# Two gated Flamingo layers in fp32: the place of a weight fold, the order of pools, the norms of the last layer and the order of two stores

## Chip, cores and metric

The kernel runs on one core of a Trainium2 chip. The metric is the time of one execution on the device in microseconds (us); lower is better. The time before is 3406.6 us, the median of three runs. All data is fp32.

## The reference, cut

`x` is 8 x 256 x 1024, `ctx` likewise. Each of four sublayers is added to `x` through a tanh gate, after a layer norm of `x`:

```python
x = x + tanh(g_xattn[0]) * L0_xattn(layernorm(x), ctx, ctx)
x = x + tanh(g_ffn[0])   * L0_ffn(layernorm(x), W, b, A, B, gate_w, gate_b)
x = x + tanh(g_xattn[1]) * L1_xattn(layernorm(x), ctx, ctx, mask, wq, wk, wv, wo)
x = x + tanh(g_ffn[1])   * L1_ffn(layernorm(x), W_base, b_base, enc0, enc1, coefs0, coefs1, mask0, mask1)

# L0_xattn: autocorrelation over 8 heads of 128 channels
qf, kf = fft(q, axis=seq), fft(k, axis=seq)
corr = ifft(qf * conj(kf)).real                  # per channel, 256 lags
w, idx = top_k(corr over lags, 11); w = softmax(w)
out = sum_i w[i] * v[min(idx[i] + pos, L - 1)]

# L0_ffn: x W^T + b, plus a LoRA path whose rank (8, 16, 32 or 64) a gate picks per token (top 1)

# L1_xattn: grouped-query attention, 32 query heads, 8 heads of keys and values, rope, mask, softmax

# L1_ffn: base linear plus 0.5 * sum over 3 experts of a real inverse Fourier
# transform of (x enc0^T) w0^T + (x enc1^T) w1^T; all of it is linear in x
```

## The kernel before

**Passes and sublayers.** The kernel makes two passes (`p` = 0 and 1) over four batches each. A pass holds its x in eight tiles of 128 x 1024 (`xt`) and runs through `autocorrelation`, `lora_ffn`, `attention` and `fourier_ffn`. Products of matrices are computed with seven block products in place of eight (`SEVEN`), so there are sums of operands (L158 on POOL or DVE, L206 to L209) and additions of results (`combine`, L220 to L250; `add_product`, L252 to L274; `residual`, L371) besides the matmuls.

**Autocorrelation.** The loop takes eight turns, one for each batch and half of the channels, and a last one that only ends the eighth. A turn transforms its half of the context and of the normalized x with matmuls against a constant (`dft<-...`, L412), multiplies spectra (L428 to L431 on DVE, then L432 to L436 on POOL), transforms back (`ps_cor`, L562 and L563) and picks the eleven best lags on DVE (`lags`, L574 to L587). POOL adds and subtracts the two halves of the weights (`both`, L553). The next turn turns these over with PE (`pt<-ident,both`, L513), transforms them (L412), multiplies them with the spectrum of the values, and adds the result to x (`po`, L532, and `residual` L371). So in each turn there is the front half of one piece and the back half of the one before.

**What runs beside it.** PE would often wait in these turns, so the turn calls `fill(n)`, which pulls n steps from the generator `beside()` (L1167). Its steps are pieces of other work, mostly matmuls: `keys_values(n)` for the two blocks of 512 context tokens of the pass (56 steps each: matmuls L798 for k and v from the weights `wk` and `wv` and the context tiles `cx`, whose sums `cx_t` are formed on POOL at L158 for block 1), and in pass 0 `fold_last_layer` (17 steps). The fold makes one weight of the whole last sublayer: masked coefficients on DVE and POOL, eight steps of matmuls L302 with the Fourier matrix, then eight steps of matmuls L320 (40 rows deep), whose results are added to `w1` on DVE (L327), summed for the seven products (L333 to L336 on DVE) and stored to device memory (L332, L338). What steps are left after the last turn are run behind it (L1189). In pass 0 there are 129 steps; the turns pull 122 of them, and seven steps of the fold are left.

**Tiles and order.** The wide tiles lie in a pool of seven buffers for each of three tags (`a`, `b`, `xn`): weights, context tiles and the fold's operands share these buffers, and a load waits until the tile before in its buffer is done with. The other pools are opened by each stage; a later pool lies over the place of an earlier one, and with `reuse_waits="tile"` an instruction that writes a tile waits for the users of whatever tiles lay at that place. So the order in which a stage opens its pools sets which tiles of the next stage lie over which tiles of this one. Each engine works through its own list in order; SP issues the loads and direct stores, also in order. A scheduler puts the instructions into these lists, so calls that are moved in the code can also move others.

**The layer after it.** `lora_ffn` starts with its norms (`xn`, L356), transposes (L366, copies `xnT` L367 on ACT), the gate and LoRA product (`pa<-ag,xnT`, L625) and then the wide products (L669). Its operand `ag` is loaded at L1207.

**The last layer.** `fourier_ffn` (L1090) loads the folded weight, computes the statistics of all eight tiles (`norm_stats`: L349, L350, L351, L352), and then for pairs of tiles `m`: normalizes and transposes both (`prepare`), forms the operands' sums (`left`), and runs the seven products of the pair before (`project`, matmuls L1127). At the end of `project`, the even tile of x goes to the output with a direct store from SP (L1136), and the odd one with a scatter by row numbers from POOL (L1137). Both write the same output tensor, and the second of them waits for the first.

Of the kernel before, what the change touches and what calls it, by code (L numbers as in the profile page):

```python
# [19 lines left out]
P = 128  # L20
B, S, D = 8, 256, 1024
# [3 lines left out]
TT = BP * S // P  # L25
# [8 lines left out]
NBT = NB // P  # L34
# [12 lines left out]
def flamingo_kernel(ctx: ExitStack, tc: tile.TileContext, a: dict, out: bass.AP):  # L47
# [336 lines left out]
    def autocorrelation(p, xt, pools, beside, late):  # L384
# [88 lines left out]
        def turn(this, before, coming):  # L473


            after = None
            if this:
                b, cols, end, qe, qo, ke, ko = this
                if coming:
                    coming = loads(coming)  # L480
                kr_ps, ki_ps = dft((KCE, ke)), dft((KSE, ko), (NYQ, ke))


                kr, ki, kn = sb("kr"), sb("ki"), sb("kn")
                nc.scalar.copy(kr, kr_ps)
                nc.scalar.copy(kn, kr_ps)
                nc.scalar.activation(ki, ki_ps, AF.Copy, scale=pair)
                nc.scalar.copy(kn[0:1, :], ki_ps[0:1, :])
                re, im = sb("re"), sb("im")
                products(spectrum((CE, SE), (qe, qo)), kr, ki, kn, re, im, False)  # L490
                fill(2)

            if this:
                vr_ps, vi_ps = dft((KCO, ko)), dft((KSO, ke))
                vr, vi = sb("vr"), sb("vi")
                nc.scalar.copy(vr, vr_ps)
                nc.scalar.copy(vi, vi_ps)

                nc.vector.scalar_tensor_tensor(
                    kr[0:1, :], end[0:1, :], 2.0 * S, kr[0:1, :], ALU.mult, ALU.add  # L500
                )
                fill((1 if p == 0 else 2) if before else 6 if p == 0 else 2)
            last = not this
            if before:
                if last:
                    fill(3)
                b_cols, b_tiles, (bkr, bki, bkn, bvr, bvi, both) = before

                wt = []
                for t in range(2):  # L510
                    pt = ps_out.tile([P, HALF], F32, tag="out", name="pt")
                    for c in range(4):
                        nc.tensor.transpose(pt[:, c * P : (c + 1) * P], both[:, t, c, :], ident)  # L513
                    wt.append(one(f"wt{t}"))
                    nc.scalar.copy(wt[t], pt)
                    fill(2 if last else 1)
                er, ei = sb("re"), sb("im")
                products(spectrum((CE, SE), wt), bkr, bki, bkn, er, ei, True)
                fill(2 if last else 1)
                odr, odi = one("odr"), one("odi")  # L520
                products(spectrum((CO, SO), wt[::-1]), bvr, bvi, bvr, odr, odi, True)
                fill(3 if last else 2)
            if this and coming:
                after = sums(*coming)

            def back(l):


                if before:
                    po = ps_out.tile([P, HALF], F32, tag="out", name="po")  # L530
                    for i, (k, sp) in enumerate(((0, er), (3, odi)) if l else ((1, ei), (2, odr))):
                        nc.tensor.matmul(po, inv2[:, k, :], sp, start=(i == 0), stop=(i == 1))  # L532
                    residual(b_tiles[0][:, b_cols], po, tg_x[0])
                    residual(b_tiles[1][:, b_cols], po, tg_x[0] if l else ntg_x[0])
                    fill(1 - l)

            if last:
                back(0)
                back(1)
                return None, None  # L540
            w = big_tile("xn", [4, S], "w")
            cor = correlation(re, im, 0)
            fill(1)
            back(0)
            cor += correlation(re, im, 2)
            for c in range(2):
                lags(w[:, c, :], cor[c])
            fill(1)
            back(1)
            for c in range(2, 4):  # L550
                lags(w[:, c, :], cor[c])
            both = big_tile("xn", [2, 4, P], "both")
            nc.gpsimd.tensor_add(both[:, 0], w[:, :, 0:P], w[:, :, P:S])  # L553
            nc.gpsimd.tensor_sub(both[:, 1], w[:, :, 0:P], w[:, :, P:S])
            return after, (cols, xt[b * 2 : b * 2 + 2], (kr, ki, kn, vr, vi, both))
# [534 lines left out]
    def fourier_ffn(p, xt, groups):  # L1090
        with (
            tc.tile_pool(name="f1c", bufs=1, reuse_waits="tile") as w1,
            tc.tile_pool(name="f1", bufs=2, reuse_waits="tile") as w2,
            tc.tile_pool(name="f1_t", bufs=4, space=PSUM) as ps_t,
            tc.tile_pool(name="f1_o", bufs=4, space=PSUM) as ps_o,
        ):
            w = stored_weight(groups, lambda r: w1_d[WEIGHTS.index(r)])

            bias1 = w1.tile([P, D], F32, name="bias1")
            nc.sync.dma_start(bias1, a["b1"].partition_broadcast(P))  # L1100
            nc.vector.tensor_scalar(bias1, bias1, tg_f[1], None, ALU.mult)
            norms = [norm_stats(xt[i * NBT : (i + 1) * NBT]) for i in range(TT // NBT)]

            def prepare(t):
                xn = w2.tile([P, D], F32, tag="xn", name="xn")
                normed(xn, xt[t], *norms[t // NBT], t % NBT)
                xnT = w2.tile([P, KC, P], F32, tag="xnT", name="xnT")
                transposed(xnT, xn, ps_t, "t")
                return xnT

            def left(first, second):
                q = [[s[:, k * KH : (k + 1) * KH, :] for k in range(2)] for s in (first, second)]
                s = [w2.tile([P, KH, P], F32, tag=f"s{i}", name=f"s{i}") for i in (1, 2, 4)]
                return left_operands(nc.vector, q, *s)

            def project(m, ops):
                x = [
                    [xt[m * 2 + i][:, j * HALF : (j + 1) * HALF] for j in range(2)] for i in range(2)
                ]
                part = [w2.tile([P, HALF], F32, tag=f"part{i}", name=f"part{i}") for i in range(2)]  # L1120

                for i in range(2):
                    nc.vector.tensor_add(xt[m * 2 + i], xt[m * 2 + i], bias1)
                for r in SEVEN:
                    po = ps_o.tile([P, HALF], F32, tag="o", name="po")
                    for c in range(KH):
                        nc.tensor.matmul(  # L1127
                            po,
                            ops[r][:, c, :],
                            w[r].chunk(c),  # L1130
                            start=(c == 0),
                            stop=(c == KH - 1),
                        )
                    add_product(r, po, x, tg_f[1], ntg_f[1], part)
                b = p * BP + m
                nc.sync.dma_start(out[b * S : b * S + P, :], xt[m * 2])  # L1136
                nc.gpsimd.indirect_dma_start(  # L1137
                    out,
                    bass.IndirectOffsetOnAxis(ap=rows[:, b : b + 1], axis=0),
                    xt[m * 2 + 1],  # L1140
                    None,
                )

            pending = None
            for m in range(TT // 2):
                got = left(prepare(m * 2), prepare(m * 2 + 1))
                if pending is not None:
                    project(*pending)
                pending = (m, got)
            project(*pending)  # L1150

    for p in range(NPASS):
        ga, gb = ("a", "b") if p % 2 == 0 else ("b", "a")
        xt = [xpool.tile([P, D], F32, tag="x", name="x") for t in range(TT)]
        with (
            tc.tile_pool(name="kv1", bufs=1, reuse_waits="tile") as kw1,
            tc.tile_pool(name="kv2", bufs=2, reuse_waits="tile") as kw2,
            tc.tile_pool(name="ac1", bufs=1, reuse_waits="tile") as c1,
            tc.tile_pool(name="acw", bufs=1, reuse_waits="tile") as aw1,
            tc.tile_pool(name="ac2", bufs=2, reuse_waits="tile") as aw2,  # L1160
            tc.tile_pool(name="ac_dft", bufs=4, space=PSUM) as ps_dft,
            tc.tile_pool(name="ac_cor", bufs=1, space=PSUM) as ps_cor,
            tc.tile_pool(name="ac_out", bufs=1, space=PSUM) as ps_out,
# [3 lines left out]
            def beside():  # L1167
                for n in range(p * BP * S // NB, (p + 1) * BP * S // NB):
                    yield from keys_values(n, (ga, gb), (kw1, kw2, ps_kv))
                if p == 0:  # L1170
                    yield from fold_last_layer((ga, gb), (kw1, ps_kv))

            def load_x(tiles):
                for t in tiles:
# [182 lines left out]
```

## Time and profile before

| | |
|---|---|
| median of 3 runs | 3406.6 us (3405.16 to 3411.6) |
| the profiled execution | 3400.72 us |
| its span, first to last instruction | 3399.0 us |
| mean granted clock of TensorE | 0.989 |
| DMA, mean over the span | 126 GB/s |

PE is the engine for matmuls (PEld its weight loads, which overlap), DVE, ACT and POOL work on elements, SP issues DMAs. A row of a timeline gives start, duration, engine, line, operation, out<-in, the partitions and elements, how many instructions were joined, and in brackets how long the engine had been idle and what ended that. "PEclk" is the clock that PE was granted, in tenths of full speed (1.00 in windows is full). The costliest groups of the page, for the sizes of things:

```profile
L954 PE MATMUL po<-wo,oT 128*128 128x512 f32 x960 | 432.1, 593 | 0.0
L925 PE MATMUL ps_q<-xn,wq 128*128 128x256 f32 x1920 | 428.9, 379 | 0.0
L371 DVE SCALAR_TENSOR_TENSOR x<-po,tg,x 128x512 f32<-128x512 f32 x376 | 269.0, 745 | 201.3 <-PE po L954 70.6
```

The columns behind the bar are busy time in all, the mean duration of one in ns, and the engine's idle time just before them. Durations of matmuls overlap one another; their distance from start to start is what counts.

### The profile page before, as it was taken

The numbers are of one execution on the slowest core, as the hardware profiler recorded it, in microseconds if no ns is written. First come the engines' busy times: TensorE is split into PE (matmuls) and PEld (weight loads), VectorE is DVE, ScalarE is ACT, GpSimd is POOL, SyncE is SP. The second block draws the span as 40 slices with busy tenths as digits, with TensorE's granted clock in tenths as the row PEclk, the third lists the DMA queues.
The fourth block names the chain that finished last, engine by engine and source line by source line (L and its number), as shares of the span: only waits on it lengthen the run. The fifth ranks groups of instructions, "written<-read, shape, count | busy, mean of one in ns | idle before, by whom it ended". The sixth has DMA issues, their size and how long they took to land. (4 is left out here: it accounts for less than half of the span.)

```text
span 3399.0 us, 36938 instructions
## 1 busy us (share of the span) xinstructions
PE 3319.6 (98%) x12784; PEld 2281.0 (67%) x12784; DVE 2245.2 (66%) x4229; ACT 859.5 (25%) x2061; POOL 1355.3 (40%) x1211
## 2 busy tenths in 40 slices
PE   8999999999999999999999999999999999999998
PEld 6676456777667767775467766577767777776754
DVE  7787666877777766665657775566666666666662
ACT  1332111322232322222123321122222323222220
POOL 4655212434443443445345541123443443344432
PEclk9999899999999999999999999999999999999999
DMA  7533625333333333343164333143333333333411
GB/s 273 172 115 117 213 87 176 118 137 133 139 126 129 121 119 120 121 163 103 50 203 153 126 102 131 32 158 123 123 121 121 113 123 115 121 123 122 152 38 50
DMA packets 161864, 431.72 MB, mean 127 GB/s; under 512 B 21476, under 2 KB 56292, under 8 KB 161678
## 3 DMA queue, kind: packets, MB, share of 16 engines
q1 hardware_dynamic: 160526, 425.17, 37.1%
q0 software_dynamic: 1152, 4.19, 0.3%
q8 instruction: 102, 1.67, 0.2%
q14 instruction: 84, 0.69, 0.1%
HBM read 350.66 MB, written 78.64 MB: 126 GB/s over the span
## 5 line engine op out<-in xcount | busy, mean ns | idle before, releaser
L719 POOL TENSOR_TENSOR qT<-rope,rope 128x512 f32<-128x512 f32 x128 | 170.0, 1328 | 866.9 <-DVE rope L718 866.9
L954 PE MATMUL po<-wo,oT 128*128 128x512 f32 x960 | 432.1, 593 | 0.0
L925 PE MATMUL ps_q<-xn,wq 128*128 128x256 f32 x1920 | 428.9, 379 | 0.0
L371 DVE SCALAR_TENSOR_TENSOR x<-po,tg,x 128x512 f32<-128x512 f32 x376 | 269.0, 745 | 201.3 <-PE po L954 70.6
L925 PEld LDWEIGHTS ps_q<-xn,wq 128*128 128x128 f32 x1920 | 364.8, 190 | 50.4 <-PE po L678 0.5
L987 ACT ACTIVATE s<-s,nmx 128x256 f32<-128x256 f32 x512 | 255.9, 500 | 276.5 <-DVE nmx L984 276.0
L982 DVE COPY_PREDICATED s<-keep,ps_s 128x512 f32<-128x512 uint8 x256 | 186.2, 730 | 183.0 <-PE ps_s L973 179.6
L954 PEld LDWEIGHTS po<-wo,oT 128*128 128x128 f32 x960 | 177.4, 190 | 175.6 <-issue 170.5
L954 PE MATMUL po<-wo,oS 128*128 128x512 f32 x640 | 287.7, 592 | 0.3 <-DVE x L371 0.3
L925 PE MATMUL ps_q<-xn_t,wq 128*128 128x256 f32 x1280 | 285.6, 379 | 0.0
L1014 ACT COPY wT<-pt 128x512 f32<-128x512 f32 x256 | 138.2, 590 | 516.3 <-PE pt L1008 516.0
L925 PEld LDWEIGHTS ps_q<-xn_t,wq 128*128 128x128 f32 x1280 | 243.2, 190 | 33.0
L1019 PE MATMUL av<-wT,v 128*128 128x256 f32 x1024 | 247.7, 384 | 3.8 <-ACT wT L1014 3.6
L973 PE MATMUL ps_s<-kT,qT 128*128 128x256 f32 x1024 | 247.9, 379 | 0.0
L1019 PEld LDWEIGHTS av<-wT,v 128*128 128x128 f32 x1024 | 192.5, 191 | 79.2 <-issue 44.0
L996 DVE TENSOR_SCALAR s<-s,tot 128x256 f32<-128x256 f32 x512 | 219.6, 469 | 7.7
L981 POOL MEMSET s<- 128x512 f32 x256 | 129.9, 527 | 222.2 <-PE pt L1008 220.5
L954 PEld LDWEIGHTS po<-wo,oS 128*128 128x128 f32 x640 | 119.0, 190 | 136.6 <-issue 128.9
L973 PEld LDWEIGHTS ps_s<-kT,qT 128*128 128x128 f32 x1024 | 191.6, 190 | 25.3 <-DVE x L371 0.5
L258 POOL TENSOR_TENSOR x<-x,part 128x512 f32<-128x512 f32 x80 | 114.9, 1436 | 213.5 <-ACT part L257 193.6
L984 DVE TENSOR_REDUCE nmx<-s 128x2 f32<-128x512 f32 x256 | 175.0, 685 | 8.3
L716 DVE TENSOR_TENSOR rope<-c,tab_q 128x512 f32<-128x512 f32 x128 | 88.4, 691 | 125.8 <-POOL c L240 119.9
(255 smaller groups left out, 5599.4 us busy)
## 6 DMA issues: line engine op xcount, KB each, us to landing
wq<-in_wq_dram SPq DMA_DIRECT2D x104, 512.0 KB, 3.3
wo<-in_wo_dram SPq DMA_DIRECT2D x104, 512.0 KB, 3.5
wq<-wq_d SPq DMA_DIRECT2D x96, 512.0 KB, 3.2
wo<-wo_d SPq DMA_DIRECT2D x96, 512.0 KB, 3.2
w<-w_d SPq DMA_DIRECT2D x36, 512.0 KB, 4.7
wk<-in_wk_dram SPq DMA_DIRECT2D x26, 512.0 KB, 5.8
wv<-in_wv_dram SPq DMA_DIRECT2D x26, 512.0 KB, 4.4
wk<-wk_d SPq DMA_DIRECT2D x24, 512.0 KB, 4.4
```

The costliest lines, as they stand in the source:

```text
L371: nc.vector.scalar_tensor_tensor(xs, ps, g, xs, ALU.mult, ALU.add)
L719: nc.gpsimd.tensor_add(dst, t0, t1)
L925: nc.tensor.matmul(ps[:, l, :], wops[r][:, l, c, :], xo[r][:, c, :], start=(c == 0), stop=(c == KH - 1),)
L954: nc.tensor.matmul(po, ops[r][:, h, t * P : (t + 1) * P], wops[r][:, h, :], start=(h == 0), stop=(h == 1),)
L973: nc.tensor.matmul(ps[:, t, :], qT[i, n][:, l, t * P : (t + 1) * P], kT[:, n * S : (n + 1) * S], start=True, stop=True,)
L981: nc.gpsimd.memset(s, MASKED)
L982: nc.vector.copy_predicated(s, keep[b], ps)
L984: nc.vector.tensor_reduce(nmx, s, AX.X, ALU.max, negate=True)
L987: nc.scalar.activation(s[:, t, :], s[:, t, :], AF.Exp, bias=nmx[:, t : t + 1], accum_out=tot[:, t : t + 1],)
L996: nc.vector.tensor_scalar(s[:, t, :], s[:, t, :], tot[:, t : t + 1], None, ALU.mult)
L1014: nc.scalar.copy(wT[i], pt)
L1019: nc.tensor.matmul(av[:, i, :], kv[step][1][:, n * 2 + c, :], wT[i][:, c, :], start=(c == 0), stop=(c == 1),)
```

## The change

Four edits, in the order of the diff:

1. In `turn`, the number of steps that are pulled after the transforms of the values (L502) is 2 in turns with a piece before them, in pass 0 too (it was 1 there). In `beside()`, the fold comes behind the first block of keys and values instead of behind the second. So in pass 0 the turns pull 129 steps, and the fold's 17 are steps 57 to 73, which fall into the fourth and fifth turn; the second block has steps 74 to 129.
2. In `fourier_ffn`, the statistics are computed for a block of four tiles when the first of them is prepared, instead of for all eight tiles at the start.
3. In `project` of `fourier_ffn`, the scatter of the odd tile is called ahead of the direct store of the even one.
4. The two pools of the keys and values (`kv1`, `kv2`) are opened behind the three pools of the autocorrelation instead of ahead of them.

Lines behind L1102 of the new kernel have numbers that are larger by two (L1127 is L1129); L1136 and L1137 trade places (L1144 and L1138).

```diff
@@ -499,7 +499,7 @@
                 nc.vector.scalar_tensor_tensor(
                     kr[0:1, :], end[0:1, :], 2.0 * S, kr[0:1, :], ALU.mult, ALU.add
                 )
-                fill((1 if p == 0 else 2) if before else 6 if p == 0 else 2)
+                fill(6 if p == 0 and not before else 2)
             last = not this
             if before:
                 if last:
@@ -1099,9 +1099,11 @@
-            norms = [norm_stats(xt[i * NBT : (i + 1) * NBT]) for i in range(TT // NBT)]
+            norms = {}
 
             def prepare(t):
+                if t % NBT == 0:
+                    norms[t // NBT] = norm_stats(xt[t : t + NBT])
                 xn = w2.tile([P, D], F32, tag="xn", name="xn")
                 normed(xn, xt[t], *norms[t // NBT], t % NBT)
                 xnT = w2.tile([P, KC, P], F32, tag="xnT", name="xnT")
@@ -1133,13 +1135,13 @@
                 b = p * BP + m
-                nc.sync.dma_start(out[b * S : b * S + P, :], xt[m * 2])
                 nc.gpsimd.indirect_dma_start(
                     out,
                     bass.IndirectOffsetOnAxis(ap=rows[:, b : b + 1], axis=0),
                     xt[m * 2 + 1],
                     None,
                 )
+                nc.sync.dma_start(out[b * S : b * S + P, :], xt[m * 2])
@@ -1153,11 +1155,11 @@
         with (
-            tc.tile_pool(name="kv1", bufs=1, reuse_waits="tile") as kw1,
-            tc.tile_pool(name="kv2", bufs=2, reuse_waits="tile") as kw2,
             tc.tile_pool(name="ac1", bufs=1, reuse_waits="tile") as c1,
             tc.tile_pool(name="acw", bufs=1, reuse_waits="tile") as aw1,
             tc.tile_pool(name="ac2", bufs=2, reuse_waits="tile") as aw2,
+            tc.tile_pool(name="kv1", bufs=1, reuse_waits="tile") as kw1,
+            tc.tile_pool(name="kv2", bufs=2, reuse_waits="tile") as kw2,
@@ -1167,8 +1169,8 @@
             def beside():
                 for n in range(p * BP * S // NB, (p + 1) * BP * S // NB):
                     yield from keys_values(n, (ga, gb), (kw1, kw2, ps_kv))
-                if p == 0:
-                    yield from fold_last_layer((ga, gb), (kw1, ps_kv))
+                    if n == 0:
+                        yield from fold_last_layer((ga, gb), (kw1, ps_kv))
 
             def load_x(tiles):
```

## The prediction

> **What bounds the kernel now.** I read the page first (busy times, forty slices, chain), then PE's waits and the stretches around its idle time.
>
> ```profile
> PE 3319.6 (98%) x12784; PEld 2281.0 (67%) x12784; DVE 2245.2 (66%) x4229; ACT 859.5 (25%) x2061; POOL 1355.3 (40%) x1211
> PEclk9999899999999999999999999999999999999999
> ```
>
> PE is the bound; the change removes no matmul. So only PE's waits and its slow clock can move the time. From the start-to-start times of back-to-back matmuls (109 ns for 128x128, 215 for 128x256, 429 for 128x512) I get 3263 us of matmul work in the 3399.0 us span; some 121 us lie between and within them. The edits touch four of these places.
>
> First, the end of pass 0's autocorrelation, where the fold's last L320 matmuls run. Columns: window, sum, PE, PEld, DVE, ACT, POOL busy, granted clock, DMA share, GB/s.
>
> ```profile
> 390.00:400.00 10.00, 9.58 (x34) 4.49 (x32) 7.88 (x14) 1.07 (x2) 0.00 (x0) 0.92 0.86 278
> 400.00:410.00 10.00, 10.00 (x15) 3.96 (x14) 6.83 (x11) 0.00 (x0) 0.00 (x0) 0.50 0.64 245
> 410.00:420.00 10.00, 6.27 (x16) 3.23 (x15) 8.60 (x27) 1.17 (x2) 0.00 (x0) 0.50 0.79 286
> 420.00:430.00 10.00, 9.18 (x34) 6.65 (x34) 7.62 (x26) 2.28 (x6) 0.00 (x0) 0.71 1.02 372
> ```
>
> PE is "busy" here at half clock: 27.3 us of it, from 398.4 on. PE's own timeline of the place:
>
> ```profile
> 401.51 12.45 PE L320 MATMUL acc<-dec,encr 40*128 40x512 f32 x14
> 417.69 1.94 PE L366 MATMUL pt<-ident,xn 128*128 128x128 f32 x8 [3.73 <-DVE sc L636]
> ```
>
> Second, the same place in pass 1 (DVE, then ACT, then PE):
>
> ```profile
> 2079.36 0.80 DVE L356 TENSOR_SCALAR xn<-x,mv,rstd 128x1024 f32<-128x1024 f32 x1
> 2083.94 0.81 DVE L356 TENSOR_SCALAR xn<-x,mv,rstd 128x1024 f32<-128x1024 f32 x1 [3.77 <-DMA v_d<-v]
> ...
> 2085.10 0.29 ACT L351 ACTIVATE rstd<-mv,eps 128x2 f32<-128x2 f32 x1 [11.40 <-DVE mv L350]
> 2085.31 1.05 ACT L367 COPY xnT<-pt 128x512 f32<-128x512 f32 x2
> ...
> 2085.92 3.68 PE L625 MATMUL pa<-ag,xnT 128*128 128x68 f32 x16 [4.61 <-ACT xnT L367]
> ```
>
> The second xn overlays a keys/values tile whose store has to land; behind it stand the statistics, behind those rstd on ACT, behind that the copies that PE awaits. A half-clock stretch of 6.8 us follows. Third, the start of the last layer:
>
> ```profile
> 3280.85 0.73 DVE L371 SCALAR_TENSOR_TENSOR x<-po,tg,x 128x512 f32<-128x512 f32 x1
> 3281.50 1.28 DVE L349 BATCH_NORM_STATS2 st<-x 128x6 f32<-128x512 f32 x2
> ...
> 3282.81 0.76 DVE L356 TENSOR_SCALAR xn<-x,mv,rstd 128x1024 f32<-128x1024 f32 x1
> ...
> 3283.71 1.94 PE L366 MATMUL pt<-ident,xn 128*128 128x128 f32 x8 [3.55 <-DVE xn L356]
> ```
>
> Fourth, the end; below it the window in which the fourth turn lies (columns as above) and the largest group of DVE work that the fold brings there:
>
> ```profile
> 3390.80 0.33 SPq L1136 DMA_DIRECT2D out_dram<-x  x1
> ...
> 3394.21 0.97 POOL L1137 DMA_INDIRECT out_dram<-x,rows  x1 [11.17 <-DMA out_dram<-x]
> ```
>
> ```profile
> 200.00:250.00 50.00, 48.62 (x182) 33.41 (x181) 43.30 (x110) 17.40 (x33) 25.25 (x18) 1.00 0.34 108
> ...
> L327 DVE TENSOR_TENSOR w1in<-w1in,acc 128x512 f32<-128x512 f32 x16 | 10.8, 683 | 6.7 <-PE acc L320 6.7
> ```
>
> **The change, part by part.** The fold's place is the only cost of size.
>
> *A, fold in turns 3 and 4 of pass 0.* Both blocks of keys and the fold are pulled in steps, 129 in all; with two steps at L502 in every later turn all are used up inside the eight turns, and the fold's 17 fall into the fourth and fifth. There PE has little else, DVE much. From the fourth turn's first correlation (L562) to the last L320, PE has in its new order 9 correlation matmuls of 0.43 (3.9), 16 L320 (13.7), 4 L532 (3.4) and 11 L412 (9.5) of 0.86 each, and 8 transposes L513 (0.9): 31.4 us. DVE has, in its order ahead of the last L327: four lag sets of 2.45 (9.8), 29 L327 and L333 to L336 at 0.61 start to start (17.7), four L371 at 0.67 (2.7), five products L428 to L431 at 0.60 (3.0), L499 and one L349 (1.4): 34.6; it begins 2.3 us in, when ACT has copied the correlation, and I allow 2.5 for two holes in which it waits for PE. That is 39.4, so PE is some 8 us late here. Then comes a chain: SP issues the load of cx_11 for block 1 only behind the store of the last w1in (0.7 us of issues, landing 3.8, the median of cx); POOL, in order, has six context sums L158 of 1.26 behind it (7.6), then odr L432 (1.26); PE's po<-odr L532 waits for that: 39.4 + 0.7 + 3.8 + 7.6 + 1.3 = 52.8. PE without any wait would be there at 31.4 + 3.0 (rest of the correlation) + 0.9 + 1.7 = 37.0. Stall 15.8; I add 3 for half clock after such idles (this trace: 3.87 idle, then 3.4 us at half clock; 5.5 idle, then 6.8), with nothing off for the 0.9 of waits that the old order had at 232 and 240. **+19.** Bounds: +8 if the sums find cx_11 landed early and only DVE counts; +28 if holes double and the seven wk loads behind cx_11 (512 KB each; the trace's best ten microseconds moved 372 GB/s, so 1.4 us each) come late too.
>
> *B, the end of pass 0 without the fold.* Before, 350 to 450 loses 22.1 us: 13.65 by the half clock (27.3 / 2), 4.4 ahead of L366 at 417.69, 1.4 at 364.5, the rest small. After, this end should look like pass 1's with part C: a wait of some 2.3 for both L553, 3.3 for L140 and L371 ahead of xn, 1.0 to 1.7 for ag (issued only behind the last v_d store, landing 4.9 to 5.8 later), half clock for 3.4 to 6.8 us (1.7 to 3.4 lost): 9 to 11.5. **−12**, bounds −9 and −14. The cover is whatever DVE does meanwhile; if ag lands last, 1.7 more is lost, inside the bound.
>
> *C, order of pools.* In pass 1 the second xn no longer waits 3.77 for the store; the copies L367 come ahead of rstd on ACT. ag is issued at some 2075.9 instead of 2079.89 and lands at 2081 to 2081.7. pa starts there instead of at 2085.92: −4 to −5, and up to −3.4 if the 6.8 us at half clock go with the idle time. **−6**, bounds −8 and −2 (ag's landing at the top of its range and the dip stays). At pass 1's start the keys/values tiles now lie elsewhere; the rows there show no wait on them, 0.
>
> *D, norms by block.* xn follows L371 at once: 3281.5 for 3282.81, −1.3 in each pass; the dips behind these waits (3.4 us in pass 0, 6.8 in pass 1) lose 1.7 and 3.4. What moves behind it, the second block's statistics (four tiles of two L349 at 0.64 and an L350 at 0.2, 5.9 us of DVE) and a table load of 1.28 on ACT, lies beside the first products L1127, seven of 3.4 us a pair of tiles; were DVE full there, it would be late by as much again. **−5**, bounds −2.6 and −8.
>
> *E, scattered store first.* At the end, the odd tile is ready at 3388.0, while the direct store waits until 3390.80; the scatter now starts at 3388.05 and needs some 3.35 to land, 3391.4, and the direct one, in write order behind it, lands 2.64 later: 3394.1 for 3397.56 before. **−3.4**, bounds −2.5 and −3.5. SP is moved to wait on the scatter: at the end of pass 0 that is about 0.65 us for what is queued behind it there (the cn load and through it ke and ko, which feed the first L412). Before, PE has no wait there beyond 1.0 at 1726.40; **+0.3**, bounds 0 and +0.7.
>
> Sum: 19 − 12 − 6 − 5 − 3.4 + 0.3 = −7.1, against the profiled run's 3400.7, that is −0.21%. The profiled run lies 5.9 under the median 3406.6 (3405.16 to 3411.6), which I take as a constant offset: 3406.6 − 7.1 = 3399.5.
>
> A rule bears on this: the Trainium skill, "TensorE: Matmul & The Clock Gate", Part 1, says that PE idle gaps over some 3.4 us cost the clock and shorter ones do not. This trace has a full clock after 3.53 and 3.85 idle, half clock after 2.64, and 27.3 us of half clock with no such gap ahead of it. By the rule alone the stretch at 398 has no cause, and A's waits would cost clock only where one of them passes 3.4 us whole; cut into shorter ones they would cost none of the 3, and the sum would be some −10.
>
> **The rivals.**
>
> 1. *The half clock moves with the fold* (slower). The 27.3 us began while 40-row L320 matmuls and 68-column L625 ones shared PE, without an idle gap. If L320 is its cause, then with sixteen L320 spread over 39 us of the fourth and fifth turn PE may run at half clock for 34 us, losing 17 where I put 0 beyond the 3 for idles: −7.1 + 17 = +9.9, 3416.5. It decides from some 7 us lost. For it: no other row names a cause for that stretch. Against: full matmuls lie between, the L302 matmuls, whose result has 40 rows, ran at clock 1.00, and DVE is the later engine there, so part of the loss hides.
> 2. *The fold is hidden* (faster by more). If DVE keeps up (no holes, no feedback through the two accumulator banks) and cx_11's load comes early because its buffer is free, A is +7: −19, 3387.5. For it: DVE was 43.30 busy of 50 at 200 to 250, with keys' work that now comes later. Against: the sum of its queue above.
> 3. *The ends stay as they are.* C, D and half of B bring nothing since something else is late at the same time (ag for C, the other statistics for D): −7.1 + 6 + 3.5 + 4 = +6.4, about 3413.
>
> **How the numbers follow.** Some 0.2% (6.8 us) is what a measurement here can tell from no change. Forecast 0.40 with its own range 3392 to 3405 (0.26 faster, 0.13 same, 0.01 slower); rival 1 0.28 (0.06 same, 0.22 slower); rival 2 0.22, all faster; rival 3 0.10 (0.06 same, 0.04 slower). Sums: faster 0.48, same 0.25, slower 0.27. The range runs from near rival 2 to near rival 1, 3385 to 3415.
>
> **What would show it.** A: PE idle ahead of po<-odr between some 270 and 310, POOL in L158 before it, DVE full; clock there. B: no half clock of 27 us at the end of pass 0. C: pa<-ag within 2.5 us of the transposes. D: xn right behind L371. E: the direct store last, landing some 2.6 after its issue. I am wrong if the clock row shows a long stretch of half speed in the fourth and fifth turn, or if SP's loads of wk set PE's pace behind it.

## The result, and the profile after

| | before | after |
|---|---|---|
| median, runs of both on one chip | 3409.51 us (3404.9 to 3412.87, 14 runs) | 3412.0 us (3408.13 to 3415.31, 14 runs) |
| the profiled execution | 3400.72 us | 3411.12 us |
| its span | 3399.0 us | 3409.3 us |
| mean granted clock of TensorE | 0.989 | 0.987 |

The ratio is 1.0006, with a 95% interval of 0.9997 to 1.0014: no change that can be measured, and surely not the forecast gain of 0.21%. The profiled execution of before was a quick one; a second trace of the same kernel, taken for the experiments, has a span of 3407.9. Below, "before" is two traces where two numbers stand.

To see where time went I sum, for every matmul, its distance to the next start less the distance that bounds the shortest tenth of its form: waits, half clock and issue together ("lost", in us; a wait counts where the matmul behind it starts). The 3263 us of work are the same in all traces.

| stretch | before, two traces | after | difference from their mean |
|---|---|---|---|
| 100 to 200: second and third turn of pass 0 | 2.8, 2.4 | 11.9 | +9.3 |
| 200 to 300: the fold's new place (part A) | 9.1, 9.3 | 25.0 | +15.8 |
| 300 to 460: end of pass 0's autocorrelation (B) | 23.2, 27.3 | 16.6 | −8.7 |
| 1610 to 1700: last layer, pass 0 (D) | 5.9, 8.2 | 5.0 | −2.0 |
| 1700 to 2050: turns of pass 1 | 20.5, 20.9 | 25.3 | +4.6 |
| 2050 to 2150: end of pass 1's autocorrelation (C) | 12.2, 12.5 | 7.0 | −5.4 |
| from 3200: last layer, pass 1 (D) | 7.0, 7.2 | 4.5 | −2.6 |
| last matmul to the end (E) | 8.96, 8.97 | 5.26 | −3.7 |

The parts that were forecast sum to −6.6 (forecast −7.1). The two other stretches, which no part of the forecast priced, took 13.9. With −1.3 in the stretches not listed that makes the +6 between the spans (3409.3 and the mean of 3399.0 and 3407.9).

The chain of part A in the changed kernel's timelines (DVE, SP, POOL, then PE). Columns as in the prediction: start, duration, engine, line, what.

```profile
246.65 0.68 DVE L327 TENSOR_TENSOR w1in<-w1in,acc 128x512 f32<-128x512 f32 x1
...
247.36 0.36 SPq L338 DMA_DIRECT2D w_d<-w1in  x1
247.77 0.46 SPq L732 DMA_DIRECT2D cx<-in_ctxT_dram  x1
...
248.01 1.68 POOL L432 TENSOR_TENSOR re<-ma,mb 128x512 f32<-128x512 f32 x1 [10.08 <-DVE mb L429]
249.65 3.39 POOL L158 TENSOR_TENSOR cx_t<-cx,cx 128x512 f32<-128x512 f32 x2
...
254.25 2.94 POOL L158 TENSOR_TENSOR cx<-cx,cx 128x512 f32<-128x512 f32 x2
257.15 2.49 POOL L158 TENSOR_TENSOR cx_t<-cx,cx_t 128x512 f32<-128x512 f32 x2
259.60 2.48 POOL L158 TENSOR_TENSOR cx_t<-cx_t,cx 128x512 f32<-128x512 f32 x2
262.04 1.26 POOL L432 TENSOR_TENSOR odr<-ma,mb 128x512 f32<-128x512 f32 x1
...
254.35 1.95 PE L532 MATMUL po<-im,inv 128*128 128x512 f32 x2 [3.92 <-POOL im L434]
263.36 2.08 PE L532 MATMUL po<-odr,inv 128*128 128x512 f32 x2 [4.37 <-POOL odr L432]
```

The last sum on DVE, the store, the load of cx_11 (the last of the block's four context tiles) behind it, six context sums on POOL, odr, and PE waiting for it: the order that was forecast. One link of it did not bind: the load landed at 251.99, and the sums that read cx_11 start at 254.25, when POOL is through with what it could begin only at 248.01, after 10.08 us of waiting for DVE. So DVE's delay reached PE through POOL's own row, and without the load the time would have been the same as far as this trace shows. From the fourth turn's first correlation (204.27) the last L327 ends 43.1 us later (forecast 39.4) and po<-odr starts 59.1 later (forecast 52.8). PE's two waits here are 3.92 and 4.37. Of the 200 to 300 stretch 20.5 us lie at half clock, 10.2 of them (230.6 to 240.8) ahead of the last L327; that this makes the difference from the forecast times is likely, but no run shows it.

What was not forecast stands in the second turn. DVE, then POOL, then PE:

```profile
128.02 6.28 DVE L584 SCALAR_TENSOR_TENSOR w<-took,ex 128x256 f32<-128x256 f32 x1
134.23 0.74 DVE L371 SCALAR_TENSOR_TENSOR x<-po,tg,x 128x512 f32<-128x512 f32 x1
...
127.85 1.29 POOL L463 TENSOR_TENSOR qe<-xn 128x512 f32<-128x512 f32 x1
129.10 1.26 POOL L464 TENSOR_TENSOR qo<-xn 128x512 f32<-128x512 f32 x1
130.32 1.26 POOL L158 TENSOR_TENSOR wv_s<-wv_s,wv 128x512 f32<-128x512 f32 x1
131.54 2.48 POOL L158 TENSOR_TENSOR wv_s<-wv,wv_s 128x512 f32<-128x512 f32 x2
...
135.69 2.08 PE L532 MATMUL po<-re,inv 128*128 128x512 f32 x2 [6.37 <-DVE x L371]
```

The same L584 in the first trace of before:

```profile
129.54 1.37 DVE L584 SCALAR_TENSOR_TENSOR w<-took,ex 128x256 f32<-128x256 f32 x1
```

L584, an instruction that takes 0.43 us in the median, took 6.28: as long as POOL's unbroken row of additions and subtractions lasts (it ends at 134.02). Behind it stands L371, which empties PSUM for PE. PE waits 6.37 us, and the clock is at half for 10.2 us from 131.6 on; PE works through some 6 of these, which cost it 3.

The other three places, after. End of pass 0 (DVE, PE), end of pass 1 (PE), start of the last layer (DVE, PE), last stores (POOL, SP):

```profile
432.45 1.40 DVE L371 SCALAR_TENSOR_TENSOR x<-po,tg,x 128x512 f32<-128x512 f32 x2
433.77 1.54 DVE L356 TENSOR_SCALAR xn<-x,mv,rstd 128x1024 f32<-128x1024 f32 x2
...
434.72 1.94 PE L366 MATMUL pt<-ident,xn 128*128 128x128 f32 x8 [5.49 <-DVE xn L356]
...
2102.88 1.09 PE L366 MATMUL pt<-ident,xn 128*128 128x128 f32 x8 [0.50 <-DVE xn L356]
2105.51 1.97 PE L625 MATMUL pa<-ag,xnT 128*128 128x68 f32 x16 [1.54 <-DMA ag<-in_ag_dram]
...
3297.50 0.73 DVE L371 SCALAR_TENSOR_TENSOR x<-po,tg,x 128x512 f32<-128x512 f32 x1
3298.15 1.52 DVE L356 TENSOR_SCALAR xn<-x,mv,rstd 128x1024 f32<-128x1024 f32 x2
...
3299.10 3.56 PE L366 MATMUL pt<-ident,xn 128*128 128x128 f32 x16 [2.29 <-DVE xn L356]
...
3402.38 0.97 POOL L1138 DMA_INDIRECT out_dram<-x,rows  x1 [5.24 <-DVE x L371]
...
3405.76 0.33 SPq L1144 DMA_DIRECT2D out_dram<-x  x1
```

At the end of pass 0 PE waits 5.49 us with nothing left to do; at the end of pass 1 the two waits are 0.50 and 1.54 where they were 1.56 and 4.61; in the last layer xn follows L371 at once and PE waits 2.29 for 3.55; the scatter goes first, and the direct store is issued when it has landed.

### The profile page after: what moved, and what is told of

Same layout as the page of the kernel before. It is cut to its first block, busy times and chain, and to the rows that moved or that the text cites. A ratio compares the mean times of both kernels' runs of the same rounds, so it can differ in the third digit from the quotient of the medians.

```text
span 3409.3 us, 36925 instructions
## 1 busy us (share of the span) xinstructions
PE 3327.1 (98%) x12784; PEld 2282.3 (67%) x12784; DVE 2254.1 (66%) x4229; ACT 860.6 (25%) x2061; POOL 1353.3 (40%) x1211
## 5 line engine op out<-in xcount | busy, mean ns | idle before, releaser
L371 DVE SCALAR_TENSOR_TENSOR x<-po,tg,x 128x512 f32<-128x512 f32 x376 | 269.2, 745 | 199.0 <-PE po L954 70.5
L996 DVE TENSOR_SCALAR s<-s,tot 128x256 f32<-128x256 f32 x512 | 219.5, 469 | 7.7
L716 DVE TENSOR_TENSOR rope<-c,tab_q 128x512 f32<-128x512 f32 x128 | 88.5, 691 | 125.8 <-POOL c L240 119.9
```

What stands on the lines that cost most here:

```text
L371: nc.vector.scalar_tensor_tensor(xs, ps, g, xs, ALU.mult, ALU.add)
L996: nc.vector.tensor_scalar(s[:, t, :], s[:, t, :], tot[:, t : t + 1], None, ALU.mult)
```

## The experiments

Three theories are set against each other. H (hold): the gain went into DVE instructions that were held behind rows of POOL additions in the turns, and the second step at L502 brings these holds about. E (end): it went at the end of pass 0, where the second step leaves no matmuls for the boundary. N (noise): the trace of before was a lucky one, and the places cost and bring something else than the two traces say.

Ratios are to the kernel before, which ran on the same chip beside each kernel (21 to 23 runs of it). Its median moved between 3406.4 and 3411.7 with the chip, so ratios count, not times.

**The first edit alone** (the kernel before with it)

```diff
-                fill((1 if p == 0 else 2) if before else 6 if p == 0 else 2)
+                fill(6 if p == 0 and not before else 2)
...
-                if p == 0:
-                    yield from fold_last_layer((ga, gb), (kw1, ps_kv))
+                    if n == 0:
+                        yield from fold_last_layer((ga, gb), (kw1, ps_kv))
```

> The kernel before with the first edit alone (fold behind the first block of keys, two steps in every turn). Theory H (held DVE): by the two traces the edit costs 16 us of PE time between 200 and 300 us, and 9 more between 100 and 200, where one DVE instruction L584 took 6.28 us behind an unbroken row of POOL instructions; it brings back 4 to 8 at the end of pass 0. Time 3421 to 3427, 12 to 17 above before. Rival N (noise): the profiled execution of before was a fast one (3400.7, median 3409.5), the 9 us are chance, and the fold's place alone costs 16 and brings 8 to 12: 3413 to 3418. The prediction on record had 19 against 12 for it: 3416.

Measured: 3416.41, ratio 1.0027 (1.0015 to 1.0040), +9 us: between H (12 to 17) and N (4 to 8), and near the forecast's own number (19 − 12). Its trace has the held L584 again (6.26 us), and loses 10.2, 23.7 and 15.8 in the first three stretches of the table above.

**The other three edits alone** (the changed kernel with the first edit undone)

> The changed kernel with the first edit undone: order of pools, norms by block and order of stores remain. Theory H: these bring what the traces show at their places, 4.8 + 3.4 + 3.7 = 12 us: 3397 to 3399. Rival N: the places shift time only, and the end of the kernel alone is sure (3.7): 3405 to 3407. Prediction on record: 6 + 5 + 3.4 less 0.3, 3395.

Measured: 3401.53, ratio 0.9985 (0.9976 to 0.9994), −5 us: nearer to N than to H. The places themselves do what they did in the changed kernel (from 3200 on 4.5 lost, last matmul to the end 5.26; 2050 to 2150: 9.5, with PE waiting 3.08 for ag), but at the end of pass 0 nothing was gained: 28.2, with 30.7 us of half clock, as the fold still lies there.

**One step instead of two at L502, the fold in its new place** (the changed kernel with one line of before)

```diff
-                fill(6 if p == 0 and not before else 2)
+                fill((1 if p == 0 else 2) if before else 6 if p == 0 else 2)
```

> The changed kernel with one step instead of two at L502 in pass 0: the fold stays between the two blocks, but every turn behind the first pulls one step less, so seven steps of the second block's values are left behind the last turn. Theory H: POOL's row and DVE's order in the second turn are those of before, L584 there takes under 1.5 us, the 9 us go: 3399 to 3404, and full matmuls stand at the end of pass 0. Rival N: 3409 to 3414, as the changed kernel.

Measured: 3385.67, ratio 0.9942 (0.9928 to 0.9955), −20 us, far beyond both theories. One step per turn is worth some 22 us here. Its trace against the changed kernel's: 6.8 for 11.9 at 100 to 200, 18.9 for 25.0 at 200 to 300, 7.0 for 16.6 at 300 to 460: together 20.8 of the 21.7 by which the spans differ. L584 took 2.61 (H expected under 1.5). At 200 to 300, in the fold's own turns, the half clock is 20.5 us in both traces; it is PE's waits that shrink, from 11.3 to 5.0, and why they do was not followed further. The end of pass 0, on PE:

```profile
413.18 3.62 PE L798 MATMUL ps_v<-wv,cx 128*128 128x256 f32 x16
416.63 1.04 PE L366 MATMUL pt<-ident,xn 128*128 128x128 f32 x8
417.91 2.00 PE L625 MATMUL pa<-ag,xnT 128*128 128x68 f32 x16 [0.24 <-ACT xnT L367]
```

The seven steps left over put 12 us of full matmuls (from 404.55) between the last turn's L532 and the next sublayer's transposes. DVE does L371 and xn meanwhile, PE waits 0.24 instead of 5.49, and no slow clock follows.

**The sums of the second value weight on DVE instead of POOL** (the changed kernel, with one line of `made_weight` changed)

```diff
-                eng = Short(nc.gpsimd if kind == "wv" else nc.vector)
+                eng = Short(nc.gpsimd if (kind, u) == ("wv", 0) else nc.vector)
```

> The changed kernel with the operand sums of the second value weight (block 0, ten instructions L154 and L158) on DVE instead of POOL: DVE gets some 6 us more work there, PE's order is the same. Theory H: POOL's row is broken, L584 in the second turn falls from 6.28 to under 2 us and PE's wait of 6.4 us with its 10 us of half clock goes, less what DVE's added work delays: 3403 to 3408. Rival N: DVE gets later by its added work, 3413 to 3418.

Measured: 3401.57, ratio 0.9988 (0.9979 to 0.9997), some 6 us less than the changed kernel's 1.0006. L584 takes 0.43 us there, and 100 to 200 loses 6.8 for 11.9: a better time with more work on the busier engine. As H had it in direction and size.

**One step less in the second turn alone** (the changed kernel with one line changed)

```diff
-                fill(6 if p == 0 and not before else 2)
+                fill(6 if p == 0 and not before else 1 if (p, b, cols.start) == (0, 0, HALF) else 2)
```

> The changed kernel with one step instead of two at L502 in the second turn of pass 0 alone (the turn in which L584 took 6.28 us); all later steps come one step later, one step is left behind the last turn. Theory H: POOL's row there is that of before, L584 takes under 3 us, PE's wait of 6.4 us and the half clock behind it go: 7 to 9 less than the changed kernel, 3400 to 3404. Rival E (end): what the one-step variant gained came from the seven steps left at the end of pass 0; with one step left the time is within 3 of the changed kernel's, 3407 to 3412.

Measured: 3409.59 (3398.66 to 3419.3, 12 runs), ratio 1.0013 (1.0003 to 1.0023). A miss for H: no gain. But the runs lie 20 us apart, and the profiled one, the quickest, has no hold. So it ran once more.

> The variant with one step in the second turn alone, once more, for a second trace: its first trace was its fastest of twelve runs (3398.7, median 3409.6). Theory H: a hold of some 4 to 9 us of one DVE instruction that the first trace didn't have, in pass 0 or 1, and half clock behind it, make up the 10 us. Rival: no hold; more half clock at the same waits.

Measured: 3414.52 us, span 3412.7 against 3396.9. The same program, in the first trace (DVE) and in the second (DVE, PE):

```profile
122.25 1.59 DVE L584 SCALAR_TENSOR_TENSOR w<-took,ex 128x256 f32<-128x256 f32 x1
```

```profile
121.80 11.44 DVE L584 SCALAR_TENSOR_TENSOR w<-took,ex 128x256 f32<-128x256 f32 x1
...
135.08 2.08 PE L532 MATMUL po<-re,inv 128*128 128x512 f32 x2 [6.82 <-DVE x L371]
```

1.59 us in one run, 11.44 in the other, both times beside an unbroken row of POOL instructions. A second L584, at 256.73, took 8.62, and an L716 5.10. Lost at 100 to 200: 5.8 and 11.6; at 300 to 460: 21.3 and 30.0. So the hold is real, and 5.8 us more are lost at its place, near the 7 to 9 that H gave it; but the number of steps in that turn doesn't decide it: one program has it in one run and not in the next.

**No step at L502 in the last three turns of pass 0** (the changed kernel with one line changed)

```diff
-                fill(6 if p == 0 and not before else 2)
+                fill(6 if p == 0 and not before else 0 if p == 0 and (b == 3 or (b, cols.start) == (2, HALF)) else 2)
```

> The changed kernel with no step instead of two at L502 in the sixth, seventh and eighth turn of pass 0: six steps of the second block's values are left behind the last turn; the first five turns are those of the changed kernel. Theory H alone: L584 still takes 6 us in the second turn, no gain beyond 2 us: 3407 to 3412. Theory E: PE has full matmuls while DVE does the last lags, L371 and xn; of the 14.5 us lost between 350 and 450 some 10 go: 3398 to 3402. If both hold, this and the run with the second turn alone add up to the 23 us by which the one-step variant beats the changed kernel, as far as the fold's own turns don't change.

Measured: 3405.91, ratio 0.9993 (0.9984 to 1.0002), 4 us less than the changed kernel: between the theories. L584 is held as before (6.30 us). From 350 to 460 it loses 6.0 less than the changed kernel (9.0 for 15.0), but from 300 to 350, in turns with no steps to fill them, 2.9 more. E's 10 did not come.

**One step at L502 in both passes** (the one-step variant with one line changed)

```diff
-                fill((1 if p == 0 else 2) if before else 6 if p == 0 else 2)
+                fill(1 if before else 6 if p == 0 else 2)
```

> The one-step variant (3385.7, 0.9942 of before) with one step at L502 in pass 1 as well, so that seven more steps are left at the end of pass 1. Theory E: the waits and the half clock at 2050 to 2095 (9 us in the one-step variant's trace) go for the most part: 3378 to 3381. Rival: the turns of pass 1 lose the cover of these seven steps, and the waits come back there: 3384 to 3390.

Measured: 3382.21 (3376.2 to 3389.22), ratio 0.9929 (0.9917 to 0.9941); 0.9942 without it. The intervals overlap, so a gain of 4 us is likely rather than shown; but its place is clear: 2050 to 2150 loses 1.0 where the one-step variant lost 6.5. It is the quickest version of this study.

Its trace shows something else as well. Up to 1769 us PE, DVE, ACT and POOL have the same instructions in the same order as in the one-step variant, the fold's L320 among them, at 210 to 245 us there and 210 to 237 here. The window 220 to 230 (columns as in the prediction), first of the one-step variant, then of this one:

```profile
220.00:230.00 10.00, 10.00 (x12) 2.78 (x11) 6.73 (x12) 0.59 (x1) 0.00 (x0) 0.50 0.96 350
220.00:230.00 10.00, 10.00 (x26) 4.04 (x24) 10.00 (x17) 0.36 (x1) 2.52 (x2) 1.00 1.03 373
```

The one has 13.7 us of half clock among the L320, the other none. So the L320 alone don't set the clock.

**The kernel before, a second trace**

> The kernel before, once more, for a second trace of it: which of its waits come again. Theory H: L584 in the second turn takes under 3 us in this trace too (1.37 in the first one), as the order of DVE and POOL there is the same. Rival N: such holds come and go from run to run, and one over 4 us shows in this trace at another place in the first 250 us. Span 3399 to 3408.

Measured: span 3407.9, no DVE instruction in the first 250 us held by more than 1.2 us, so H's part holds. The 8.9 us against the first trace come from the clock: 37.5 us at half speed at the end of pass 0 for 27.3, and 104.5 in all for 73.9.

**The fold's place alone** (the kernel before with this edit)

```diff
                 for n in range(p * BP * S // NB, (p + 1) * BP * S // NB):
                     yield from keys_values(n, (ga, gb), (kw1, kw2, ps_kv))
-                if p == 0:
-                    yield from fold_last_layer((ga, gb), (kw1, ps_kv))
+                    if n == 0:
+                        yield from fold_last_layer((ga, gb), (kw1, ps_kv))
```

> The kernel before with the fold's place alone: behind the first block of keys, with one step at L502 as before, so seven steps of the second block's values stand at the end of pass 0. With the kernel before (0), the first edit whole (+10) and the run below this makes a table of two by two. Theory H+E: the one-step variant was 20.7 below before, the other three edits alone 5 below, so the place alone brings some 15: 3391 to 3396. Rival: the one-step variant's gain needs the new order of pools at the end of pass 0 (xn not behind the keys' and values' stores there): 3398 to 3404.

Measured: 3413.84, ratio 1.0011 (1.0002 to 1.0020). The rival is right, and more so than it said: without edits 2 to 4 the place brings nothing, and at the end of pass 0 the trace points to the order of pools. Its end of pass 0 (DVE, PE), with the same seven steps last:

```profile
417.72 0.68 DVE L244 TENSOR_TENSOR v<-ps_v,u 128x512 f32<-128x512 f32 x1
421.73 0.80 DVE L356 TENSOR_SCALAR xn<-x,mv,rstd 128x1024 f32<-128x1024 f32 x1
422.72 0.82 DVE L356 TENSOR_SCALAR xn<-x,mv,rstd 128x1024 f32<-128x1024 f32 x1 [0.18 <-DMA v_d<-v]
...
422.58 1.97 PE L366 MATMUL pt<-ident,xn 128*128 128x128 f32 x8 [7.52 <-DVE xa L640]
```

xn comes behind the keys' and values' last work L244, and the second one waits for their store, since it lies over their tile. PE waits 7.52 us where the one-step variant, with the other order of pools, has no wait. Against that variant this trace loses 10.5 us more at 300 to 460, the end of pass 0, which edits 2 and 3 don't touch; the other 13 lie where C, D and E lie.

**The second step alone** (the kernel before with this edit)

```diff
-                fill((1 if p == 0 else 2) if before else 6 if p == 0 else 2)
+                fill(6 if p == 0 and not before else 2)
```

> The kernel before with two steps instead of one at L502 in pass 0 alone; the fold stays last, but all of it is used up inside the last turns, none is left behind. Theory H: L584 in the second turn takes some 6 us again and PE loses some 9 us at 100 to 150: 3413 to 3420. Theory E (only the end matters): the fold's L320 no longer lie beside the start of the next sublayer; their half clock of 27 us shrinks, and the end loses what the changed kernel's lost, 10: within 5 of before.

Measured: 3408.46, ratio 0.9992 (0.9983 to 1.0001). L584 is held (6.26 us), 100 to 200 loses 9.1, as H had it; but 200 to 300 loses 2.8 where before lost 9.1 and 9.3, so the sum is nothing: E's time, by another way. The half clock with the fold's L320 did not shrink (44.4 us at 300 to 460), against E's expectation.

The runs in one table, ratio to before:

| place of the fold | steps at L502 | edits 2 to 4 | ratio |
|---|---|---|---|
| last | 1 | no | 1 |
| last | 2 | no | 0.9992 |
| last | 1 | yes | 0.9985 |
| middle | 1 | no | 1.0011 |
| middle | 2 | no | 1.0027 |
| middle | 2 | yes (the changed kernel) | 1.0006 |
| middle | 1 | yes | 0.9942 |

Each interval reaches some 0.001 to either side. The eighth, the fold last with two steps and edits 2 to 4, was not run.

**POOL and DVE alone**

```python
for i in range(8):
    nc.gpsimd.tensor_add(c[i], c[i - 1] if dependent and i > 0 else x, y)   # 128x512 each
work(c[0])     # on DVE, beside additions 2 to 8
```

The kernel holds seven such sections; the rest of the computation is left out.

> Only rows of eight POOL additions of 128x512 (two inputs in SBUF) with one kind of DVE work started behind the first of them; the whole computation of the reference is left out, and x goes to the output. Seven sections: (1) additions independent of one another, DVE the instruction of L584 (128x256, two SBUF inputs, accumulator); (2) each addition reads the one before; (3) as 1, with one DVE input in PSUM; (4) as 1, three DVE products 128x512; (5) as 2, three products; (6) as 1, a DVE tensor_scalar of one SBUF input; (7) as 1 again. Theory H: in 1 and 7 the DVE instruction ends only with the row, 7 additions of 1.23 us later: 8 to 9 us long; in 2, where POOL waits for its own result, it gets in after one: under 2 us; in 3 it isn't held: 0.4 to 0.5 us. Rival: it gets in between any two additions: under 2 us in 1 as well, and the 6.28 us have another cause.

Measured: H's 8 to 9 us did not come, the rival holds. DVE, of the sections 1, 2, 3, 4 and 6, then POOL's row of section 1:

```profile
6.20 1.47 DVE L39 SCALAR_TENSOR_TENSOR w<-c,y 128x256 f32<-128x256 f32 x1 [0.78 <-POOL c L32]
...
16.71 0.43 DVE L39 SCALAR_TENSOR_TENSOR w<-c,y 128x256 f32<-128x256 f32 x1 [1.37 <-POOL c L32]
...
28.13 0.42 DVE L44 SCALAR_TENSOR_TENSOR w<-pv,c 128x256 f32<-128x256 f32 x1 [1.37 <-POOL c L32]
...
38.46 5.07 DVE L50 TENSOR_TENSOR w<-c,y 128x512 f32<-128x512 f32 x3 [1.37 <-POOL c L32]
...
62.48 1.47 DVE L53 TENSOR_SCALAR w<-c 128x512 f32<-128x512 f32 x1 [1.37 <-POOL c L32]
```

```profile
4.90 9.97 POOL L32 TENSOR_TENSOR c<-x,y 128x512 f32<-128x512 f32 x8 [4.46 <-DVE y L22]
```

With two inputs in SBUF the DVE instruction waits until POOL's addition of that moment ends, 1.05 us, then gets in while the row goes on (section 7, the same again, has 1.47 too); beside additions that depend on one another, where POOL pauses between two of them, and with one input in PSUM it doesn't wait at all; three products in a row get in one by one (1.69 each); a tensor_scalar with one input in SBUF takes 1.47 as well. So a row of POOL additions by itself doesn't hold DVE to its end.

## Where the prediction was right and where it was wrong

The range held the time (3412.0 in 3385 to 3415); the likeliest case, faster by 0.21%, did not come. That the time fell into the range is owed to the range's width: the priced parts came near their sum (−6.6 for −7.1), and 13.9 us in stretches that had no price, or a price of 0, took it back. By its own steps:

- **A, the fold's place: right in place and nearly in sum, wrong in its shares.** +15.8 lost for a forecast of +19, which was 15.8 of waits and 3 of half clock. Of the measured 15.8, waits are some 6 (11.3 for 5.7 and 5.1) and half clock some 6.5 (17.6 us of PE's work at half speed for 3.4 and 5.6); the rest is small gaps. That the sum came near is luck: the waits were some 10 less than forecast, the half clock and the small gaps some 7 more. The link over cx_11's load did not bind, as told above. Rival 1 was right in kind, with 6.5 us where the prediction put 3, but short of the 7 beyond these from which it decides, and far from its 17. Its cause is not shown: half clock lay among the L320 in nine of thirteen traces (27.3 and 37.5 us where the fold is last, 10.2 at 230 to 241 in its new place, with no idle time over 1.2 us ahead of it), but the two programs with the same pass 0 had 13.7 us of it and none. What sets the clock there stays open.
- **B, the end of pass 0: right in kind, −8.7 for −12.** The bound was −9, so the gain lies just outside. The two xn stand behind L371, and L371 behind L140 and L244 in DVE's order; 10.2 us of half clock come with PE's wait where 3.4 to 6.8 were counted. The items listed in the prediction sum to 8.3 to 10.7, not to 9 to 11.5.
- **C: −5.4 for −6; D: −2.0 and −2.6, together −4.6 for −5; E: −3.7 for −3.1.** Right in place, and each within some 0.6 of its size.
- **The step that failed: "with two steps at L502 in every later turn all are used up inside the eight turns".** The second step was put at nothing. It is half of the first edit. Alone it costs nothing that was measured (0.9992), but with the fold in the middle and the other edits it costs some 22 us (1.0006 against 0.9942). Two prices were found. In the second turn, the shifted order of POOL and DVE came with a held L584 in all four traces of kernels that have the second step there and POOL's work unmoved (6.26 to 6.30 us; at most 2.61 in the six traces with one step in all later turns of pass 0), and that costs PE 6 to 10 us; but the kernel with one step in the second turn alone had the hold in one trace of two, so the link is a likelihood, not a rule. And it uses up the steps that would have stood at the end of pass 0 (16.6 lost there for 7.0). The 6 us more that are lost in the fold's own turns have no cause shown. With one step the same change is 20 us quicker than before.
- **The step that was missing: how the edits act on one another.** The sum took each edit by itself. The place alone (1.0011) and the other edits alone (0.9985) sum to −1 us and bring 20 together, since matmuls left for the end only cover xn if xn doesn't lie over the tiles that these matmuls' results go through. By the traces some 13 us of it lie there, at 300 to 460: 25.3 before (the mean of two), 17.5 with the place alone, 28.2 with the other edits alone, 7.0 with both. For the rest no cause is shown. The table of ratios can't be read as a sum.
- **Pass 1's turns, put at 0:** they lost 25.3 for 20.5 and 20.9. In six traces one L467 of pass 1 is held for 9.1 us (lost there 23.9 to 26.2), in six others, with the same instructions there and with either order of pools, it isn't (20.5 to 24.5). One program, with one step in the second turn alone, has this hold in its second trace and not in its first. So it is chance of the run as far as these traces show, not the change's doing, and by the means of the two groups it makes some 3 of the 4.6 us.
- **Rival 2** (the fold hidden) fell; **rival 3** (the ends stay) fell as a mechanism, though its time, 3413, is nearest: the ends gave what they should, and the turns took it back. Its sum doesn't follow its words either: without C, D and half of B, at the prediction's own prices, it is +9.9, not +6.4.
- **Two readings of the trace.** The idle times that the prediction gives as 3.53, 3.85 and 2.64 are 3.37, 3.69 and 2.47 in the trace's rows; half clock after 2.47 and full clock after 3.69 still stand against the rule as the prediction states it, full clock after 3.37 does not. The trace's best ten microseconds moved 406 GB/s (20 to 30 us), not 372; only A's upper bound used that.

## What to carry to other kernels

Work that fills one stage's gaps is a stock: count where it runs out, and leave some full matmuls for the boundary to the next stage, where the bound engine has nothing else; then see that the next stage's first tiles don't lie over the tiles these last matmuls still use. A "little more filling per turn" is an edit with a price like any other: it shifts every engine's order behind it. Where two edits touch one boundary, try them together and apart before adding their gains.

## What the runs showed of the hardware

A DVE instruction with two inputs in SBUF can be held for the whole of an unbroken row of POOL additions and subtractions: 6.28 us behind five of them, 9.07 behind seven, 11.44 behind ten, where it takes 0.4 to 0.7 alone. In the long holds that I followed it ended 0.3 to 0.6 us behind the row's last instruction. The Trainium skill, "SBUF — State Buffer", "SBUF: two separate sides", says that such an instruction and a GpSimd one that reads SBUF shut each other out: the one that starts first has the shared ports for the whole of its instruction. The run with the two engines alone agrees (1.47 us with two SBUF inputs, 0.42 with one in PSUM). Holds over many instructions go beyond what it says, and here the measurement decides. A tensor_scalar with one input in SBUF can be held too: L996, 0.35 us in the median, takes 2.28 to 2.29 at one place in all thirteen traces of the full kernel (1565.48 in the first of before), beside one addition and two memsets of POOL. What makes the hold last for one addition or for ten stays open: neither a row alone (1.47) nor the program (1.59 and 11.44 in two runs of one) settles it, and the starts within POOL's instruction, as far as the traces resolve them, don't tell the two apart.
